# Keys and values of a fifth batch made between two decoder layers, with their weights in a free part of the transposed inputs

## The chip, the cores and the metric

The kernel runs on one core of a Trainium2 chip. The metric is the device time of one execution in microseconds (us). Times of the kernel before are the median of 3 runs. TensorE is PE in the profile, VectorE is DVE, ScalarE is ACT, GpSimd is POOL and SyncE is SP.

## What is computed

Two decoder layers over x of 16 batches, 112 tokens and 256 features, all in float32. A context of 16 x 375 x 256 feeds both cross-attentions. Each step adds to x what it makes of the normalised x:

```
x = x + L0_attn(norm(x))            # linear attention, 16 heads
x = x + L0_xattn(norm(x), ctx)      # softmax attention to the context, 16 heads of 16
x = x + L0_ffn(norm(x))             # shared expert + 2 of 16 experts per token
x = x + L1_attn(norm(x))            # softmax attention, 16 heads of 64
x = x + L1_xattn(norm(x), ctx)      # the second cross-attention
x = x + L1_ffn(norm(x))             # 2 of 8 experts, limited capacity
```

The second cross-attention makes its keys and values from the context alone, so they can be made at any time once the context is there:

```
cn = layer_norm(context, g2, b2)
kv = cn @ Wkv                       # 256 x 1024
k, v = split(kv, 2)                 # 8 heads of 64 each
out = softmax((xn @ Wq) k^T / 8) v @ Wout + bout
```

## The kernel before

x stays in SBUF for the whole kernel, tokens on the partitions. `xnT` holds the normalised x transposed (128 x 2 x 1792), made new for every step. `w_all` is one large buffer that holds the weights of the stages in turn. Nearly all matrix products of the linear layers are recorded at one line, L120 (`mm_sum`).

**What is made ahead.** For four batches, `AHEAD = (0, 4, 8, 12)` (L359), keys and values of the second cross-attention are made in layer 0, at the end of its cross-attention and during the routing and the shared expert of its feed-forward step. For each of these batches, `ctx_ahead` loads the context (L226), `norm_ahead` normalises it on VectorE (L238), `c_ahead` transposes it on PE (L389) and scales it on ScalarE into a tile `acT` (L392), `k_ahead` makes a quarter of the keys (two matmuls over 375 columns, copied by ScalarE to `ak`, L401), and `v_ahead` makes a third of the values (two matmuls over 512 columns, copied to `av`, L414). After the last piece, ScalarE's DMA queue writes `ak` and `av` to the DRAM tensors `kd` and `vd` (L403, L416), 750 KB each: `ak` has 128 partitions of 6000 bytes, `av` 125 partitions of 6144 bytes. The weights Wkv lie in `w_all` at this time (`wkv_a[0]`), and that place is later needed for W_qkv of layer 1.

**The expert blocks.** Tokens are scattered to DRAM by expert (`xg`, POOL's indirect DMA, L1063) and read back in blocks of 128 rows. `blocks(0)` (L1143) runs 36 blocks, software-pipelined: step n fetches block n + 5 (L1100, SP's queue), transposes block n (L1110, copied by VectorE at L1112), multiplies block n - 1 by its expert's weights (L120), transposes its activation for block n - 2 (L1126, copied by ScalarE at L1128), and makes the output of block n - 3 (L1133), which ScalarE scales into `os` (L1135) and POOL scatters to `yo` (L1063). The order on PE and VectorE in this stage is the one written in the code. W_qkv of layer 1 is loaded in three parts of 1 MB, behind the fetches of blocks 12, 17 and 22 (L1103). Then a branch on the number of blocks used (L1161, L1162) skips the further blocks; with these inputs they are not needed. The pools of layer 0 are closed after it, and the tiles of layer 1 are put into the memory they give back.

**Layer 1.** `combine(b)` (L1528) loads the expert outputs of batch b from `yo` (L1530, SP's queue) and adds them to x (L1533); `norm_one` normalises (statistics on VectorE, the power on POOL at L242 and L243), transposes on PE (L267) and copies into `xnT` (L269). The first four batches come ahead of the self-attention; SP loads the weights of layer 1 after the fourth.

In the second cross-attention, batch b is attended to in two units of four heads: `scores` (L1461; maxima on VectorE at L1472, exponentials on ScalarE at L1473, division by the sums on POOL at L1484), `turned` (transposes of the weights, L1493) and `values` (L1509, copied by VectorE at L1516). While batch b is attended to, keys and values of batch b + 1 are made from the context (`c_piece`, `k_piece`, `v_piece`: transposes L1430, matmuls L120, copies L1440 and L1447), or, for a batch of `AHEAD`, read from `kd` and `vd` (`k_load` L1415, `v_load` L1419, SP's queue). Here too PE's order is the written one.

Of the kernel before, what the change touches and what calls it, by code (L numbers as in the profile page):

```python
# [18 lines left out]
S = 375  # L19
KC = 125  # L20
NKC = S // KC
NT = B * L
# [76 lines left out]
def tile_decoder(ctx: ExitStack, tc: tile.TileContext, t: dict, out: bass.AP):  # L99
    nc = tc.nc  # L100
# [12 lines left out]
    def bank():  # L113
        return banks.tile([128, 512], F32, tag="B", name="pT")
# [3 lines left out]
    def mm_sum(o, terms):  # L118
        for i, (l, r) in enumerate(terms):
            mm(o, l, r, start=(i == 0), stop=(i == len(terms) - 1))  # L120
# [11 lines left out]
    xnT = xp.tile([128, 2, NT], F32, tag="xnT", name="xnT")  # L132
# [22 lines left out]
    def rows_of(w):  # L155
        return w.rearrange("(c p) n -> p c n", p=128)
# [4 lines left out]
    def load_w(at, parts):  # L161

        views, o = [], at
        for w in parts:
            c, k = w.shape[0] // 128, w.shape[1]
            v = w_all[:, o : o + c * k].rearrange("p (c n) -> p c n", c=c)
            nc.sync.dma_start(v, rows_of(w))
            views.append(v)
            o += c * k
        return views  # L170
# [46 lines left out]
    def vec(i):  # L217
        return vT[:, i : i + 1]
# [5 lines left out]
    def load_ctx(cxp, b):  # L224
        cx = cxp.tile([KC, NKC, D], F32, tag="cx", name="cx")
        nc.sync.dma_start(cx, t["ctx_1024"][b].rearrange("(c p) d -> p c d", p=KC))  # L226
        return cx
# [9 lines left out]
    def normed(dst, src, mv, r):  # L237
        nc.vector.tensor_scalar(dst, src, mv, r, ALU.subtract, ALU.mult)  # L238
# [117 lines left out]

    AHEAD = (0, 4, 8, 12)  # L359
    kd = {b: dr.tile([128, 4, S], F32, tag=f"kd{b}", name=f"kd{b}") for b in AHEAD}  # L360
    vd = {b: dr.tile([KC, NKC, 512], F32, tag=f"vd{b}", name=f"vd{b}") for b in AHEAD}

# [3 lines left out]
    acxs, acTs, akv = {}, {}, {}  # L366
    wkv_a, kap = [], []


    def ctx_ahead(i):  # L370
        if i < len(AHEAD):
            acxs[i] = load_ctx(cxp, AHEAD[i])

    def norm_ahead(i):
        for j in range(NKC):
            n = AHEAD[i] * NKC + j
            normed(acxs[i][:, j, :], acxs[i][:, j, :], cmv[:, n, 0:1], cr[:, n : n + 1])


    def c_ahead(i, c):  # L380
        if c == 0:
            acTs[i] = (
                kap[0].tile([128, 2, S], F32, tag="acT", name="acT", bufs=1)
                if i % 2
                else w_all[:, 2 * WR + 4864 : 2 * WR + 4864 + 2 * S].rearrange("p (c s) -> p c s", c=2)
            )
        pt = bank()
        for j in range(NKC):
            nc.tensor.transpose(  # L389
                pt[:, j * KC : (j + 1) * KC], acxs[i][:, j, c * 128 : (c + 1) * 128], ident[:KC, :KC]  # L390
            )
        nc.scalar.activation(acTs[i][:, c, :], pt[:, :S], AF.Identity, bias=vec(10 + c), scale=vec(8 + c))  # L392
        if c == 1:
            ctx_ahead(i + 2)

    def k_ahead(i, m):
        if m == 0:
            akv[i] = kz[0] if i == 0 else kap[0].tile([128, 4, S], F32, tag="ak", name="ak")
        pk = bank()
        mm_sum(pk[:, :S], [(wkv_a[0][:, c, m * 128 : (m + 1) * 128], acTs[i][:, c, :]) for c in range(2)])  # L400
        nc.scalar.copy(akv[i][:, m, :], pk[:, :S])  # L401
        if m == 3:
            nc.scalar.dma_start(kd[AHEAD[i]], akv[i])  # L403

    def v_ahead(i, j):
        if j == 0:
            akv[i] = (
                va[0].rearrange("p j h d -> p j (h d)")
                if i == 0
                else kap[0].tile([KC, NKC, 512], F32, tag="av", name="av")  # L410
            )
        pv = bank()
        mm_sum(pv[:KC, :], [(acTs[i][:, c, j * KC : (j + 1) * KC], wkv_a[0][:, c, 512:]) for c in range(2)])
        nc.scalar.copy(akv[i][:, j, :], pv[:KC, :])  # L414
        if j == NKC - 1:
            nc.scalar.dma_start(vd[AHEAD[i]], akv[i])  # L416

    ahead = [
        f
        for i in range(len(AHEAD))  # L420
        for f in (
            [lambda i=i, m=m: k_ahead(i, m) for m in range(4)]
            + [lambda i=i: v_ahead(i, 0)]
            + [lambda i=i, c=c: c_ahead(i + 1, c) for c in range(2)] * (i + 1 < len(AHEAD))
            + [lambda i=i, j=j: v_ahead(i, j) for j in (1, 2)]
        )
    ]
    ahead = [lambda c=c: c_ahead(0, c) for c in range(2)] + ahead

    def take(n):  # L430
# [522 lines left out]
    with ExitStack() as ph:  # L953
# [140 lines left out]
        with tc.manual_schedule(engines={mybir.EngineType.PE, mybir.EngineType.DVE}):  # L1094
            xbs, xTs, cols, acts, aTs = {}, {}, {}, {}, {}

            def fetch(j):
                if j < stop:
                    xbs[j] = lp.tile([BLK, RW], F32, tag="xb", name="xb", bufs=8)
                    got = nc.sync.dma_start(xbs[j], xg[j * BLK : (j + 1) * BLK, :])  # L1100
                    after_all("xg", got)
                    i = (j - 12) // 5
                    if j in (12, 17, 22):  # L1103
                        with tc.issue_after(got.ins):
                            w_qkv.extend(load_w(2 * WR + 2048 * i, [t["L1_attn_W_qkv"][i]]))

            def turn(j):
                pt = bank()
                for c in range(2):
                    nc.tensor.transpose(pt[:, c * BLK : (c + 1) * BLK], xbs[j][:, c * 128 : (c + 1) * 128], ident)  # L1110
                xTs[j] = lp.tile([128, 2 * BLK], F32, tag="bxT", name="bxT", bufs=3)
                nc.vector.tensor_copy(xTs[j], pt[:, : 2 * BLK])  # L1112

            def up(j):
                cols[j] = nc.tensor.value_load(ebi[0:1, j : j + 1], min_val=0, max_val=(E0 - 1) * 768)
                xt = xTs.pop(j)
                pu = bank()
                mm_sum(
                    pu[:, :256],
                    [(xt[:, c * BLK : (c + 1) * BLK], ew[:, bass.ds(cols[j] + c * 256, 256)]) for c in range(2)],  # L1120
                )
                acts[j] = swiglu(lp, pu[:, :128], pu[:, 128:256], 128)

            def turn_act(j):
                pt = bank()
                nc.tensor.transpose(pt[:, :BLK], acts.pop(j), ident)  # L1126
                aTs[j] = lp.tile([128, BLK], F32, tag="aT", name="aT", bufs=3)
                nc.scalar.copy(aTs[j], pt[:, :BLK])  # L1128

            def down(j):  # L1130
                xb = xbs.pop(j)
                po = bank()
                mm(po[:, :D], aTs.pop(j), ew[:, bass.ds(cols.pop(j) + 512, D)], start=True, stop=True)  # L1133
                os_ = lp.tile([BLK, D], F32, tag="os", name="os", bufs=8)
                nc.scalar.activation(os_, po[:, :D], AF.Copy, scale=xb[:, D + 1 : D + 2])  # L1135
                to = lp.tile([BLK, 1], U32, tag="to", name="to", bufs=8)

                own = lp.tile([BLK, 1], F32, tag="own", name="own", bufs=8)
                nc.vector.tensor_scalar(own, xb[:, D : D + 1], 2.0 * NT - 0.5, float(j * BLK), ALU.is_gt, ALU.mult)
                nc.vector.tensor_tensor(to, own, xb[:, D : D + 1], ALU.add)  # L1140
                scatter("yo", yo, to[:, 0:1], os_[:, :])

            def blocks(begin):  # L1143
                for j in range(begin, begin + 5):
                    fetch(j)
                for n in range(begin, stop + 3):
                    if n < stop:
                        fetch(n + 5)
                        turn(n)
                    if begin <= n - 1 < stop:  # L1150
                        up(n - 1)
                    if begin <= n - 2 < stop:
                        turn_act(n - 2)
                    if begin <= n - 3:
                        down(n - 3)


            w_qkv = []
            stop = NB_MEAN
            blocks(0)  # L1160
        n_used = nc.values_load(used[0:1, 0:1], min_val=0, max_val=NB0)  # L1161
        with tc.If(n_used > NB_MEAN):  # L1162
            with tc.manual_schedule(engines={mybir.EngineType.PE, mybir.EngineType.DVE}):
                stop = NB0
                blocks(NB_MEAN)
    cstack.close()
    f0s.close()
    rp = pool(ctx, "route", 1)
# [128 lines left out]
    with ExitStack() as ph:  # L1297
# [243 lines left out]
        with tc.manual_schedule(engines={mybir.EngineType.PE}):  # L1541
            for b in range(4):
                got = combine(b)
# [13 lines left out]
            for n, (g, i) in enumerate(units):  # L1557
# [7 lines left out]
                if n % 2 == 0 and n // 2 + 4 < B:  # L1565
                    got = combine(n // 2 + 4)
# [79 lines left out]
    with ExitStack() as ph:  # L1646
# [143 lines left out]
        got = {}  # L1790
# [75 lines left out]
        with tc.If(n_ranks > RANKS):  # L1866
            with tc.manual_schedule(engines={mybir.EngineType.DVE, mybir.EngineType.PE}):
# [5 lines left out]
                for i in range(len(ffn1_more)):  # L1873
                    n = len(ffn1_units) + i
# [33 lines left out]
```

## Time and profile before

| what | us |
|---|---|
| median of 3 runs (lowest to highest) | 1606.19 (1604.55 to 1608.27) |
| the profiled execution | 1611.35 |
| its span, first to last instruction | 1609.6 |
| PE busy in it | 1501.8 |
| start of the block stage's first transposes on PE | 546.60 |
| last matmul of the blocks starts | 607.10 |
| first yb load on SP | 613.90 |
| first transposes of layer 1 on PE | 620.98 |
| second cross-attention, first scores to last values' copy | 949 to 1315 |

How to read the lines: a line of a timeline has the start, the duration in us, the engine, the line of the code, the operation, what it writes and reads, the shape and the count; in brackets stands the idle time of the engine before it and what ended it. In PE's lines a float32 matmul of the code counts twice. A line of a window has the stretch, its length, the busy time of PE, PE's weight loads (PEld), VectorE, ScalarE and POOL with their instruction counts, the granted share of TensorE's clock, the busy share of the DMA engines and GB/s.

### The profile page before, as it was taken

Reading aid. Unit: us, or ns where it says so; the run is one execution under the profiler, and the core shown is the slowest. Engines: PE = TensorE matmul, PEld = TensorE weight load, DVE = VectorE, ACT = ScalarE, POOL = GpSimd, SP = SyncE. Lnnn points to the kernel's source line nnn. Section 1 sums busy time; section 2 is a strip of 40 time slices with the busy share of each in tenths; the row PEclk is TensorE's granted clock in tenths of the full one; section 3 lists DMA queues with packets and bytes.
Section 4 is the critical chain, followed back from the end, with each engine's and each line's share of the span. In section 5 each row is a group of like instructions: output and inputs, shape, how many; then the busy total and the mean of one; then the engine's idle time right before and its main releaser. Section 6 shows DMA issues by size and latency. Waiting matters only on the chain.

```text
span 1609.6 us, 30346 instructions
## 1 busy us (share of the span) xinstructions
PE 1501.8 (93%) x11438; PEld 1127.5 (70%) x11438; DVE 964.1 (60%) x2649; ACT 577.9 (36%) x1437; POOL 483.1 (30%) x647
## 2 busy tenths in 40 slices
PE   7898999999988896899999989999999978999998
PEld 5776777777754585778888756666666657788786
DVE  6986777777762353976677655566575566342124
ACT  3441444444442252223333233343434323333332
POOL 5642122222115352323333344544445420000000
PEclk9999999999999897999999999999999988999999
DMA  6500322222224476200000010101010012344421
GB/s 170 143 10 21 94 67 65 67 65 65 64 76 158 130 231 214 54 24 1 1 1 2 20 56 10 49 20 48 19 30 30 1 53 79 137 178 157 147 89 48
DMA packets 84929, 116.52 MB, mean 72 GB/s; under 512 B 13433, under 2 KB 70946, under 8 KB 84778
## 3 DMA queue, kind: packets, MB, share of 16 engines
q1 hardware_dynamic: 78690, 98.25, 20.1%
q0 software_dynamic: 3312, 8.54, 1.6%
q10 hardware_dynamic: 2776, 7.72, 1.4%
q8 instruction: 95, 1.56, 0.4%
q14 instruction: 56, 0.46, 0.1%
HBM read 84.41 MB, written 22.08 MB: 66 GB/s over the span
## 4 chain that ended last, share of the span: by engine, by line
PE 76%; DVE 13%; POOL 4%; DMA 3%; issue 2%; another core or an unknown queue 1%; ACT 1%; SPq 0%; POOLq 0%; DVEq 0%; ACTq 0%
PE pT L120 49%; PE pT L785 3%; PE pT L1461 3%; PE pT L1493 2%; POOL pr L1484 2%; DVE mx L769 2%; PE pT L1509 2%; PE pT L803 2%; PE pT L767 2%; PE pT L1358 2%; PE pT L1393 2%; PE pT L1379 2%; PE pT L620 1%; DVE st L234 1%
## 5 line engine op out<-in xcount | busy, mean ns | idle before, releaser
L1484 POOL TENSOR_SCALAR pr<-pr,den 112x375 f32<-112x375 f32 x128 | 157.0, 1244 | 176.9 <-DVE den L1482 157.7
L120 PE MATMUL pT<-xnT,w_all 128*128 128x224 f32 (+2 forms) x800 | 165.3, 358 | 0.6 <-DVE xnT L269 0.5
L120 PEld LDWEIGHTS pT<-xnT,w_all 128*128 128x128 f32 x800 | 145.9, 197 | 10.2 <-issue 5.7
L794 ACT ACTIVATE pr<-pT 125x336 f32<-125x336 f32 x256 | 94.6, 456 | 126.3 <-PE pT L785 126.3
L769 DVE TENSOR_REDUCE mx<-pT 112x1 f32<-112x375 f32 x256 | 122.2, 539 | 11.3 <-PE pT L767 9.9
L1371 POOL TENSOR_TENSOR pr<-pr,den 112x448 f32<-112x448 f32 x64 | 59.9, 956 | 198.8 <-DVE den L1369 147.9
L120 PE MATMUL pT<-w_all 128*128 (+3 forms) x376 | 113.1, 453 | 1.7 <-ACT w_all L392 0.8
L120 PE MATMUL pT<-w_all,cT 128*125 128x256 f32 (+1 forms) x336 | 111.4, 475 | 0.0
L120 PE MATMUL pT<-cT,w_all 128*128 128x375 f32 x320 | 110.2, 486 | 0.0
L120 PE MATMUL pT<-w_all,xnT 128*112 128x256 f32 (+1 forms) x320 | 105.7, 477 | 1.9 <-ACT xnT L566 0.9
L120 PE MATMUL pT<-w_all,oT 128*112 128x256 f32 x448 | 106.4, 383 | 0.6 <-DVE oT L1400 0.6
L242 POOL TENSOR_SCALAR nr<-nmv 112x1 f32<-112x1 f32 x96 | 22.3, 232 | 273.7 <-DVE nmv L235 273.1
L1308 ACT COPY pT<-pT 112x448 f32<-112x448 f32 (+1 forms) x64 | 34.0, 532 | 170.9 <-PE pT L1493 88.3
L120 PEld LDWEIGHTS pT<-w_all 128*128 128x128 f32 (+2 forms) x376 | 70.2, 190 | 33.8 <-issue 4.6
L1473 ACT ACTIVATE pr<-pT,top 112x375 f32<-112x375 f32 x128 | 72.4, 572 | 56.8 <-DVE top L1472 54.4
L120 PEld LDWEIGHTS pT<-cT,w_all 128*128 128x128 f32 x320 | 59.3, 190 | 41.1 <-issue 5.8
L120 PEld LDWEIGHTS pT<-w_all,oT 128*112 128x112 f32 x448 | 75.7, 177 | 16.3 <-DVE oT L1400 1.0
L120 PE MATMUL pT<-first_in,w_all 128*128 128x192 f32 x512 | 86.6, 329 | 0.0
L120 PEld LDWEIGHTS pT<-first_in,w_all 128*128 128x128 f32 x512 | 84.4, 192 | 1.5 <-issue 0.3
L120 PEld LDWEIGHTS pT<-w_all,cT 128*125 128x125 f32 x336 | 61.1, 187 | 33.3 <-issue 22.7
L120 PEld LDWEIGHTS pT<-w_all,xnT 128*112 128x112 f32 x320 | 57.1, 183 | 35.8 <-issue 22.4
L1767 DVE SCALAR_TENSOR_TENSOR hT<-pT,vT,gt 128x192 f32<-128x192 f32 x64 | 26.7, 417 | 90.5 <-ACT gt L1766 90.4
(306 smaller groups left out, 3019.2 us busy)
## 6 DMA issues: line engine op xcount, KB each, us to landing
w_all<-in_L_ffn_w_c_fc_dram SPq DMA_DIRECT2D x12, 1024.0 KB
w_all<-in_L_ffn_w_gate_dram SPq DMA_DIRECT2D x12, 1024.0 KB
w_all<-in_L_ffn_w_c_proj_dram SPq DMA_DIRECT2D x12, 1024.0 KB
cx<-in_ctx_dram SPq DMA_DIRECT2D x32, 375.0 KB
kz<-kn SPq DMA_DIRECT2D x128, 46.9 KB
xg<-w_all SPq DMA_DIRECT2D x1, 5547.0 KB
xb<-xg SPq DMA_DIRECT2D x36, 129.0 KB
yb<-yo SPq DMA_DIRECT2D x16, 224.0 KB
```

Of the source, the lines that this page charges most:

```text
L120: mm(o, l, r, start=(i == 0), stop=(i == len(terms) - 1))
L767: mm(ps[i][:L, :S], qz[b % 2][r, g, :], kz[b % 2][r, g, :], start=True, stop=True)
L769: nc.vector.tensor_reduce(mx[b % 2][:, g, i, 16:17], ps[i][:L, :S], AX.X, ALU.max, negate=True)
L785: mm(pw[i][:KC, j * L : (j + 1) * L], kz[b % 2][r, g, j * KC : (j + 1) * KC], qm[r, :], start=True, stop=True,)
L794: nc.scalar.activation(pr[:, i, :], pw[i][:KC, : NKC * L], AF.Exp)
L803: mm(po[32 * i : 32 * i + 32, :L], va[b % 2][:, j, 4 * g + i, :], pr[:, i, j * L : (j + 1) * L], start=(j == 0), stop=(j == NKC - 1),)
L1308: nc.scalar.copy(dst, src)
L1358: mm(ps[k][:L, s * L : (s + 1) * L], q, kk, start=True, stop=True)
L1371: nc.gpsimd.tensor_tensor(pr[:, k], pr[:, k], bcast(den[:, k, :], L), ALU.mult)
L1461: mm(ps[2 * s + k][:L, :S], qTs[b // 2][rows(k), m, (b % 2) * L : (b % 2 + 1) * L], kTs[b][rows(k), m, :], start=True, stop=True,)
L1473: nc.scalar.activation(pr[:, i, :], ps[i][:L, :S], AF.Exp, bias=top[:, i : i + 1], scale=1.0, accum_out=den[:, i : i + 1],)
L1484: nc.gpsimd.tensor_scalar(pr[:, n, :], pr[:, n, :], den[:, n : n + 1], None, ALU.mult)
```

## The change

Batch 2 becomes a fifth batch made ahead (index 4 of `AHEAD`), but not with the other four. Its weights, Wkv once more, are loaded into the last 1024 columns of `xnT`, which is free between the shared expert and batch 6 of layer 1, behind the fetch of block 24. Its context is normalised at step 30 of the blocks and transposed at steps 36 and 37, where the pipeline of the blocks runs out. Its keys are made after the last block and ahead of the branch, its values after the branch, still inside the pools of layer 0. In the second cross-attention, batch 2 is then read from `kd` and `vd` like the other batches of `AHEAD`, and its pieces during batch 1 go away.

```
-    AHEAD = (0, 4, 8, 12)
+    AHEAD = (0, 4, 8, 12, 2)
...
             acTs[i] = (
                 kap[0].tile([128, 2, S], F32, tag="acT", name="acT", bufs=1)
-                if i % 2
+                if i % 2 or i == 4
...
-        mm_sum(pk[:, :S], [(wkv_a[0][:, c, m * 128 : (m + 1) * 128], acTs[i][:, c, :]) for c in range(2)])
+        mm_sum(pk[:, :S], [(wkv_a[i // 4][:, c, m * 128 : (m + 1) * 128], acTs[i][:, c, :]) for c in range(2)])
...
-        mm_sum(pv[:KC, :], [(acTs[i][:, c, j * KC : (j + 1) * KC], wkv_a[0][:, c, 512:]) for c in range(2)])
+        mm_sum(pv[:KC, :], [(acTs[i][:, c, j * KC : (j + 1) * KC], wkv_a[i // 4][:, c, 512:]) for c in range(2)])
...
                     if j in (12, 17, 22):
                         with tc.issue_after(got.ins):
                             w_qkv.extend(load_w(2 * WR + 2048 * i, [t["L1_attn_W_qkv"][i]]))
+                    if j == 24:
+
+                        wkv_a.append(xnT[:, :, NT - 1024 :])
+                        with tc.issue_after(got.ins):
+                            nc.sync.dma_start(wkv_a[1], rows_of(t["L1_xattn_Wkv"]))
...
                     if begin <= n - 3:
                         down(n - 3)
+                    if begin == 0 and n == stop - 6:
+                        norm_ahead(4)
+                    if begin == 0 and n in (stop, stop + 1):
+                        c_ahead(4, n - stop)
...
             stop = NB_MEAN
             blocks(0)
+            for m in range(4):
+                k_ahead(4, m)
         n_used = nc.values_load(used[0:1, 0:1], min_val=0, max_val=NB0)
         with tc.If(n_used > NB_MEAN):
...
                 stop = NB0
                 blocks(NB_MEAN)
+        with tc.manual_schedule(engines={mybir.EngineType.PE}):
+            for j in range(NKC):
+                v_ahead(4, j)
     cstack.close()
     f0s.close()
```

The list of pieces that layer 0 works off stays at the first four batches; the context of batch 2 is loaded when the third of them has been transposed.

More of the change, by code (lines that the diff above doesn't have):

```diff
@@ L419, in tile_decoder @@
         f
-        for i in range(len(AHEAD))
+        for i in range(4)
         for f in (
@@ L423, in tile_decoder @@
             + [lambda i=i: v_ahead(i, 0)]
-            + [lambda i=i, c=c: c_ahead(i + 1, c) for c in range(2)] * (i + 1 < len(AHEAD))
+            + [lambda i=i, c=c: c_ahead(i + 1, c) for c in range(2)] * (i < 3)
             + [lambda i=i, j=j: v_ahead(i, j) for j in (1, 2)]
```

## The prediction

> **What bounds the kernel now.** I read the page first, then three stages that the change touches: the expert blocks, the gap between the layers, and the second cross-attention.
>
> From the page: the span, PE's share, and the chain that ended last.
>
> ```profile
> span 1609.6 us, 30346 instructions
> PE 1501.8 (93%) x11438; PEld 1127.5 (70%) x11438; DVE 964.1 (60%) x2649; ACT 577.9 (36%) x1437; POOL 483.1 (30%) x647
> ...
> PE 76%; DVE 13%; POOL 4%; DMA 3%; issue 2%; another core or an unknown queue 1%; ACT 1%; SPq 0%; POOLq 0%; DVEq 0%; ACTq 0%
> ```
>
> TensorE carries 76% of the chain. So work taken off it counts where it sets the pace, and work put on it costs nothing only where it idles. The timeline of PE at the end of the blocks shows where the change puts its work:
>
> ```profile
> 607.10 1.27 PE L1133 MATMUL pT<-w_all,aT 128*128 x4
> 620.98 0.61 PE L267 MATMUL pT<-call,xn 112*128 112x112 f32 x2 [12.61 <-DVE nmv L235]
> ```
>
> PE idles 12.6 us. What ends the idle time is a chain: the last rows of the blocks are scattered to DRAM, land, are loaded back as yb (L1530), added to x, normalised and transposed. The timeline and the waits of SP's queue:
>
> ```profile
> 613.90 5.56 SPq L1530 DMA_DIRECT2D yb<-yo  x4
> ```
> ```profile
> SPq L1530 <- DMA yo<-os,to: 13.6, 1, 13.6
> ```
>
> Whatever delays the yb load at 613.90 delays all that follows: between 613.90 and 620.98 nothing else runs. That load is the point to watch.
>
> **The change, part by part.**
>
> *In the blocks: +1.3.* The 1 MB weight load is put behind the fetch of block 24, two blocks behind the third W_qkv load. In the trace W_qkv's packets run from 577.81 to 582.06 (4.25 us), and xb 23, queued behind them, lands at 582.41, 1.43 before its transpose. Xb 24 lands at 583.23; then the new 4.1 us of packets, and xb 25 (0.85) lands near 588.1, where its transpose stands at 587.10: a stall of 1.0 (bounds 0 and 1.5). PE repeats every 1.63 us without slack, so the stall stays. The three normalisations (L238, 0.41 each) ahead of block 31's copy (L1112) take 1.2 us of VectorE, which is busy 1.02 of each 1.63 (0.29, 0.15, 0.16, 0.42); the copy, needed 1.0 after it would end, comes 0.25 late: +0.3 (0 to 0.6). The extra ctx load (375 KB) follows the third context's transposes, before 500; nobody needs it before 595: 0 (at most 1).
>
> *The drain: +0.6 ahead of K.* ScalarE gets two acT (L392, 0.665 each) among the last aT and os. From 607.35 its queue is acT, aT 0.27, os 0.47, acT, os 0.47. So the second acT ends near 609.5 (block shift left out) and the last os near 610.0 instead of 608.88. That os still makes its scatter: POOL issues the last three at a 1.26 pitch, the last at 610.40.
>
> *The fill on PE.* In the second cross-attention the same pieces take, by their starts on PE (half a batch's K at 985.59, then a third of V up to the values at 989.93, all of it PE work without a gap):
>
> ```profile
> 981.65 0.86 PE L1430 MATMUL pT<-call,cx 125*128 125x125 f32 x6
> ...
> 985.59 2.69 PE L120 MATMUL pT<-cT,w_all 128*128 128x375 f32 x8
> 988.12 1.88 PE L120 MATMUL pT<-w_all,cT 128*125 128x512 f32 x4
> 989.93 1.37 PE L1509 MATMUL pT<-pT,vt 125*64 125x112 f32 x24
> ```
>
> So 0.70 for the transposes, 2.53 + 2.62 for K, 1.81 + 3.43 for V: 11.1 in all. K runs 609.5 to 614.65, its last copy (0.47) ends near 615.1. The branch is cheap: in the trace ScalarE's last os ends at 608.88 and its block-end semaphore comes at 609.49, so 0.6; the first V matmul waits for that: 615.7. V ends at 620.95, its last copy (L414, 0.585) at 621.6. The PE work itself fits the gap to within 0.1.
>
> *The new wait: this decides.* The pools of layer 0 close behind the fill, and the yb tiles come from memory that is given back there. In the built program SP's first yb load waits, beside the scatters as before, for ScalarE's last av copy and for the two DMA lanes on which batch 2's kd and vd writes land. Behind it stand on SP all of yb 1 to 3 and the L1 weights; POOL (bout), VectorE (x + yb) and PE (L267) wait for the same set. How long does a vd write take? The trace holds one nearly alone: issued at 545.90, last packet at 553.05, 7.15 us. The kd write of the same 750 KB, issued at 528.2, ended at 531.42, 3.2 us. Two windows over their packets (DMA share and GB/s stand last):
>
> ```profile
> 546.70:553.00 6.30, 5.23 (x28) 3.89 (x27) 2.98 (x10) 1.16 (x6) 0.00 (x0) 1.00 0.30 118
> ...
> 529.10:531.40 2.30, 2.30 (x7) 1.61 (x6) 0.69 (x1) 0.00 (x0) 1.88 (x2) 0.50 1.00 367
> ```
>
> The vd write keeps 0.30 of the DMA engines busy, kd all. I take 7.15, the row of the same shape; 3.2 is the other end. So vd lands at 621.65 + 7.15 = 628.8, and the yb load goes out 0.3 later, its place in the wait list: 629.1. Against 613.90 that is +15.2, with the blocks' shift **+16.5** (bounds: 12.5 with kd's 3.2; 20 with V and the restart at half clock as below).
>
> *The clock.* Granted clock is the third number from the end:
>
> ```profile
> 607.71:611.12 3.41, 0.66 (x3) 0.26 (x2) 0.00 (x0) 0.95 (x2) 2.63 (x3) 1.00 0.32 123
> 611.12:614.53 3.41, 0.00 (x0) 0.00 (x0) 0.00 (x0) 0.00 (x0) 0.25 (x1) 0.50 0.10 38
> ...
> 624.77:628.19 3.42, 3.42 (x11) 3.09 (x10) 1.22 (x4) 0.54 (x1) 1.58 (x4) 0.50 1.02 396
> 628.19:631.60 3.41, 3.41 (x20) 3.41 (x19) 0.62 (x1) 0.54 (x1) 0.00 (x0) 1.00 1.07 383
> ```
>
> A 3.41 us window with little PE work is followed by half clock, and it came back 7.2 us after PE restarted at 620.98. K and V follow a busy drain, so I give them the full clock. The 1.2 us between them may drop V's clock for a window: 0 taken, 1.7 as bound. [...] But V ends 15 us before the new restart, so PE goes cold again and the restart costs what it cost: 0.
>
> *In the second cross-attention: -5.4.* Batch 2 loses 11.1 of PE work while batch 1 is attended to. But without it POOL's weights division (L1484, 4 x 1.22 per unit) sets the pace, as it does before batch 4:
>
> ```profile
> 1039.80 4.87 POOL L1484 TENSOR_SCALAR pr<-pr,den 112x375 f32<-112x375 f32 x4 [3.95 <-DVE den L1482]
> ...
> 1041.10 0.58 PE L1493 MATMUL pT<-call,pr 112*125 112x112 f32 x3 [0.83 <-POOL pr L1484]
> ```
>
> The copies of L1516 close each unit. Batches 1 and 2 run from 978.83 to 1025.63, 46.8; batches 3 and 4, the nearest pair whose second is loaded ready, to 1067.37, 41.7: 5.1 less. Later pairs: 49.0 and 48.9 made, 42.5 and 41.5 loaded, but they hold other routing work. Pair 3 and 4 has one router matmul more (0.3): I take 5.4, bounds 4.4 and 11.1 (POOL no bound). The two loads go out on SP when the buffers come free (scores end near 960, values near 968), 20 us before they are needed; other loads pass behind them without haste.
>
> **Sum.** +16.5 - 5.4 = +11.1. The profiled execution took 1611.35 (span 1609.6 and 1.75 around it), so 1622.5; it lay 5.2 above the median of the runs, 1606.19, and by the median the forecast is **1617.3**.
>
> **Rivals.**
> 1. *The gap hides the fill* (faster). If the yb load did not wait for vd's landing, the blocks' 1.3 and the gain would be left: 1.3 - 5.4 = -4.1, so 1602.1. For it: K and V fit 12.6 us. Against: the wait stands in the built program. It turns at a hold of the yb load of 4.1 us; I find 15.2. Chance 0.04.
> 2. *Cold fill, or a slow write.* V at half clock, vd beside other traffic or a worse restart: +3 to +6 more, 1620 to 1623.5. For: clock rows above. Chance 0.14, mostly in the range.
> 3. *POOL does not limit batch 1*, or vd takes kd's 3.2: 11.1 - 5.7 = 5.4, or 11.1 - 4.0 = 7.1 more than before, so 1611.6 to 1613.3. Against: the rows of batch 4 and of vd. Chance 0.08.
> 4. *It comes out even*: the hold is half of what I find and the gain at its best. Chance 0.02.
>
> The forecast has 0.72. The range, 1611.0 to 1623.5, takes in rivals 2 and 3. What can be told from no change is 0.2%, 3.2 us: faster 0.04, within 0.02, slower 0.94.
>
> **What would show it.** In the profile of the changed kernel: the first yb load near 630 instead of 613.90, released by a vd write or by ScalarE's av copy; vd issued near 623 and 0.30 DMA share for 6 us behind it; PE idle about 15 us again, now behind V; half clock over the restart; xb 25 released by its DMA; POOL waits in batch 1 like those of batch 4, and batches 1 and 2 near 41. I am wrong if SP issues the first yb load before vd lands, or if batch 1 sheds the whole 11.1.

## The result, and the profile after

The changed kernel takes **1621.15 us** (median of 8 runs, 1613.66 to 1627.22), the kernel before, run beside it, 1605.80 (8 runs, 1603.34 to 1613.48). The ratio is 1.0081, 95% interval 1.0060 to 1.0103: **slower by 13 us** by this ratio and by 15.4 by the medians, where 11.1 were forecast. Four runs of the changed kernel lie at 1614 to 1617 us, at a mean granted clock of 0.971 to 0.974, and four at 1626 to 1627, at 0.965 to 0.968, so that the median stands between them, where no run is; both profiles that were taken of it (1615.98, and 1614.82 later) are like the first four.

The profiled execution of before reached the blocks 7 to 10 us later than those below, ahead of anything that the change touches. So stages are compared below with another profile: that of the kernel before with one word changed, which makes no difference (own_bytes_before, first experiment). All times are stretches between starts of the same instructions in the traces, in us:

| stretch | own_bytes_before | after | after again |
|---|---|---|---|
| first block's transpose to the last down | 63.90 | 65.08 | 64.58 |
| last down to the first yb load | 5.69 | **20.58** | **20.60** |
| yb load to the first scores of layer 1 | 24.81 | 25.25 | 25.76 |
| these scores, first to last | 292.99 | 293.12 | 293.40 |
| second cross-attention, batches 1 and 2 | 46.80 | **42.85** | **42.88** |
| batches 3 and 4 | 44.77 | 41.77 | 41.77 |
| first block's transpose to the end | 1065.9 | 1077.1 | 1075.0 |

The last row gives +11.2 and +9.1, against the forecast +11.1. One profile against one carries some 3 us of chance. Before's own profile takes 1062.8 over the last row's stretch, and against that it is +14.3 and +12.2. Its blocks, the first row, take 60.99, and those of l1_again (below), which has the same code up to there, 66.7. Its batches 3 and 4 take 41.75 with 3.4 us of half clock in them, where the control's 44.77 have 10.2.

First the page of after: span, PE's share, and the chain by engine.

```profile
span 1614.2 us, 30350 instructions
...
PE 1505.7 (93%) x11438; PEld 1129.8 (70%) x11438; DVE 962.7 (60%) x2646; ACT 579.6 (36%) x1440; POOL 483.6 (30%) x647
...
PE 51%; DVE 5%; POOL 4%; DMA 1%; ACT 1%; issue 1%; POOLq 0%; ACTq 0%; DVEq 0%; SPq 0%
```

PE's 93% has not moved, and the kernel is 13 us slower: the share does not tell it. The chain's shares sum to 63% where those of before summed to 100%: the walk back stopped early, so they can't be compared.

The timeline of after in the gap, all engines (start, length, engine, line, what; in brackets the idle time before, and what ended it):

```profile
602.66 5.21 PE L120 MATMUL pT<-acT,xnT 128*128 128x375 f32 x16
...
609.05 5.42 PE L120 MATMUL pT<-xnT,acT 128*125 128x512 f32 x12 [1.19 <-ACTq L1173]
609.12 0.35 ACTq L403 DMA_DIRECT2D kd<-ak  x1
...
614.51 0.58 ACT L414 COPY av<-pT 125x512 f32<-125x512 f32 x1 [1.13 <-PE pT L120]
615.12 0.50 ACTq L416 DMA_DIRECT2D vd<-av  x1
622.81 5.15 SPq L1544 DMA_DIRECT2D yb<-yo  x4
623.45 0.61 POOL L1315 DMA_DIRECT2D bout<-in_L_xattn_bout_dram  x1 [18.01 <-DMA vd<-av]
...
629.26 0.61 PE L267 MATMUL pT<-call,xn 112*128 112x112 f32 x2 [14.79 <-DVE nmv L235]
```

K (602.66) and V (609.05) fill the gap as forecast, the vd write goes out at 615.12, and for 7.7 us nothing is issued. Then yb (622.81) and bout (623.45) go out together; POOL's line names what they waited for, `vd<-av`. SP's own waits view names another releaser for the same time:

```profile
SPq L1544 <- DMA yo<-os,to: 15.6, 1, 15.6
```

That is the trap of a wait for several semaphores: the scatters (`yo<-os,to`) are in the same list, but the last was issued at 604.47. Who waits at the same moment for the same set, here POOL, helps to tell. The window over vd's packets in after (DMA share and GB/s last):

```profile
616.00:622.20 6.20, 0.00 (x0) 0.00 (x0) 0.00 (x0) 0.00 (x0) 0.00 (x0) 0.67 0.30 119
```

0.30 of the DMA engines, no engine computing: the row of the earlier vd write once more.

### The profile page after: what moved, and what is told of

Its sections match the earlier page's. It is cut to its first block, busy times and chain, and to the rows that moved or that the text cites. A ratio compares the mean times of both kernels' runs of the same rounds, so it can differ in the third digit from the quotient of the medians.

```text
span 1614.2 us, 30350 instructions
## 1 busy us (share of the span) xinstructions
PE 1505.7 (93%) x11438; PEld 1129.8 (70%) x11438; DVE 962.7 (60%) x2646; ACT 579.6 (36%) x1440; POOL 483.6 (30%) x647
## 3 DMA queue, kind: packets, MB, share of 16 engines
q1 hardware_dynamic: 79236, 100.83, 20.6%
## 4 chain that ended last, share of the span: by engine, by line
PE 51%; DVE 5%; POOL 4%; DMA 1%; ACT 1%; issue 1%; POOLq 0%; ACTq 0%; DVEq 0%; SPq 0%
PE pT L120 35%; POOL pr L1498 3%; PE pT L1475 3%; PE pT L1507 2%; PE pT L1523 2%; PE pT L1372 2%; PE pT L1407 2%; PE pT L1393 2%; PE pT L1821 1%; PE pT L1289 1%; DVE x_res L1547 1%; ACT pr L1487 1%; PE pT L1444 1%; PE pT L267 1%; POOL pr L1385 0%
## 5 line engine op out<-in xcount | busy, mean ns | idle before, releaser
L1498 POOL TENSOR_SCALAR pr<-pr,den 112x375 f32<-112x375 f32 x128 | 157.1, 1245 | 174.1 <-DVE den L1496 155.1
L120 PE MATMUL pT<-w_all,cT 128*125 128x256 f32 (+1 forms) x324 | 105.9, 471 | 0.0
L120 PE MATMUL pT<-cT,w_all 128*128 128x375 f32 x304 | 104.6, 485 | 0.0
L1322 ACT COPY pT<-pT 112x448 f32<-112x448 f32 (+1 forms) x64 | 34.1, 532 | 170.5 <-PE pT L1507 88.1
```

What stands on the lines that cost most here:

```text
L1322: nc.scalar.copy(dst, src)
L1498: nc.gpsimd.tensor_scalar(pr[:, n, :], pr[:, n, :], den[:, n : n + 1], None, ALU.mult)
```

## The experiments

The theory is that of the prediction: the yb load waits until batch 2's vd write has landed, because its tile lies in memory that layer 0's pools give back. Rivals: the fill's own work is the cost; the writes' traffic is; the second cross-attention gains nothing. A ratio is always against the kernel before on the same chip, with its 95% interval.

### The wait taken away: own_bytes, and its control own_bytes_before

```diff
-        lp = pool(ph, "a1", 2)
+        lp = pool(ph, "a1", 2, reuse_waits="tile")
```

With this a tile of layer 1's first pool waits only for the users of its own bytes, not for every user of the pools that lay there. Nothing else is edited. The control has the same line in the kernel before.

> The changed kernel, with the tiles of the second layer's first pool waiting only for the users of their own bytes. The first yb load then waits for the scatters alone; fill, writes and loads stay. Theory (the hold: the yb load waits for batch 2's vd write): the yb load goes out about 6 us behind the last down instead of 20.6, PE restarts right behind V's last matmul (near 615 in a profile like that of after, instead of 629), and the time falls by 12 to 15 from the changed kernel's, to 2 to 6 below the kernel before; if the restart finds the full clock, up to 6 more. Rival 1 (the fill's own work on PE and ScalarE is the cost, the yb load only one of several that end together): the restart moves by less than 6 and the time stays above the kernel before. Rival 2 (the yb rows are late because the writes of kd and vd take the DMA engines): the load goes out early but takes much longer than 5 us.

> The kernel before with the same one word on the pool, nothing else. It tells what that word does alone. In before the first yb load waits for the last scatter's landing and ScalarE's last os, which is done by then: every theory expects no change, 0 within 1.5 us, and the yb load about 6 us behind the last down as before.

Measured: own_bytes **1.0014** (0.9991 to 1.0038; 1607.1 against 1607.7), control 0.9997 (0.9982 to 1.0012). The yb load goes out 7.07 behind the last down instead of 20.58, and 0.67% of the 0.81% is gone, by one wait. So the wait is the cost, and the fill's work on PE is not: late_kd, below, bounds that work at 1.2 behind the last down, and ahead of it the transposes of the context add 0.4 (from block 35's transposes to the last down 4.47 instead of 4.08). Rival 1 falls. But 2 to 6 us below the kernel before were expected, and the time does not go below it. Part of this is seen in the gap. SP's and PE's timelines of own_bytes:

```profile
608.77 8.77 SPq L1544 DMA_DIRECT2D yb<-yo  x4
```
```profile
608.52 5.42 PE L120 MATMUL pT<-xnT,acT 128*125 128x512 f32 x12 [1.18 <-ACTq L1173]
618.79 0.63 PE L267 MATMUL pT<-call,xn 112*128 112x112 f32 x2 [4.85 <-DVE xn L238]
```

and the same load in the control:

```profile
609.32 4.83 SPq L1530 DMA_DIRECT2D yb<-yo  x4
```

Four loads of 224 KB hold SP for 8.77 instead of 4.83, because kd's packets (609.45 to 612.28) stand in front of them, and PE restarts 4.85 behind V. Rival 2, the traffic, has its share: from the yb load to the first scores 28.66 instead of 24.81.

### A faster vd write: v_split

```diff
-            nc.scalar.dma_start(vd[AHEAD[i]], akv[i])
+            nc.scalar.dma_start(vd[AHEAD[i]][:112], akv[i][:112])
+            nc.scalar.dma_start(vd[AHEAD[i]][112:], akv[i][112:])
```

(for batch 2 alone)

> The changed kernel with batch 2's vd write cut in two: rows 0 to 111, and rows 112 to 124. The bytes and the waits stay. Theory (the hold ends with the vd write, and that write is slow because its 125 rows go over 0.30 of the DMA engines): the two parts take about 3.5 instead of 7.15 from the issue, the yb load comes 3 to 4 us earlier and the time falls by 3 to 4. Rival 1 (the write is slow by itself, 750 KB to DRAM behind kd's): still about 7, no change. Rival 2 (the hold ends with something else than the write): the write is faster, the yb load does not move.

Measured: **1.0056** (1.0037 to 1.0075), 0.25% or 4 us better than the changed kernel's ratio, with intervals that overlap (1.0075 and 1.0060). The two parts go out at 619.41 and 619.77, their last packet ends at 623.25, and yb follows 17.2 behind the last down instead of 20.6. A window over their packets, and SP's timeline:

```profile
620.30:623.20 2.90, 0.00 (x0) 0.00 (x0) 0.00 (x0) 0.00 (x0) 0.00 (x0) 1.00 0.79 250
```
```profile
623.73 5.24 SPq L1548 DMA_DIRECT2D yb<-yo  x4
```

The same bytes at 0.79 of the DMA engines instead of 0.30. The write takes 3.84 from its first issue instead of 7.15, and the yb load comes 3.4 earlier: in the trace the dose follows, in the run times its sign does. Kd's write of 128 rows keeps 0.81 of them busy (after, 609.90 to 612.30). Why 125 rows in one write keep so few busy, and 112 with 13 beside them so many, is not shown.

### The cost alone: fill_only

```diff
-        own = [b for b in range(B) if b not in AHEAD]
+        own = [b for b in range(B) if b not in AHEAD[:4]]
```

(and the same in the two conditions that choose between making and loading a batch)

> The changed kernel with everything in the fill (weights loaded, K and V of batch 2 made and written), but the second layer makes batch 2 again by itself, as before, and does not read the written one. It shows the cost without the gain. Theory: the hold of 14.5 and the blocks' 0.6 remain and the 4 of the second cross-attention are not gained: 14 to 16 above the kernel before, 3.5 to 5 above the changed kernel. Rival (the second cross-attention gains nothing in the end, the copy of 4 is lost later): the same time as the changed kernel.

Measured: **1.0110** (1.0093 to 1.0128), 17.7 us, where 14 to 16 were expected. In its profile yb follows 20.60 behind the last down, and batches 1 and 2 take 46.81. The hold is as in the changed kernel and the loaded batch's gain is absent. In run time the two differ by 0.3%, with intervals that overlap (1.0093 and 1.0103): the sign fits the theory, the size is not settled.

### The gain alone: l1_only, and l1_again for a second profile

```diff
-            nc.sync.dma_start(kTs[b], kd[b])
+            nc.sync.dma_start(kTs[b], kd[0 if b == 2 else b])
```

(vd likewise, and batch 2 counted among those that are loaded)

> The kernel before, in which batch 2's keys and values of the second cross-attention are not made but loaded from batch 0's in DRAM: the gain without the cost. It leaves out the making of batch 2's K and V, so batch 2 attends to batch 0's context. Theory: batches 1 and 2 take 42.8 instead of 46.8 because POOL's division sets the pace, and the time falls by 4 to 5.4. Rival 1 (POOL does not set the pace): by 8 to 11. Rival 2 (what is gained there is lost behind it, the whole stage waits for something else): by less than 2.

> l1_only once more, for another profile. It leaves out the making of batch 2's K and V. Its twelve runs had a median of 1609.0, with a mean granted clock of 0.963 to 0.970 in eleven of them; the profiled one was the twelfth, 1594.3 at 0.975. Theory (POOL's division sets the pace where the next batch is loaded, PE idles there, and the granted clock falls to a half behind windows in which PE was busy less than about 2 of 3.41 us, so that the gain is paid back): the profile of a run near 1609 has more or longer half-clock stretches in the second cross-attention than that of 1594, 10 us of them or more, and the stage from the first values copy on is longer by the difference. Rival (the time is lost before the second cross-attention, in the first layer or the gap): the half-clock stretches there are the same, and the difference stands elsewhere.

Measured: l1_only **1.0013** (1.0002 to 1.0025): no gain at all, where 4 to 5.4 us were expected; l1_again one run, 1607.11 beside 1605.7. In both profiles batches 1 and 2 take what was expected, 42.93 and 41.78. So the work is saved where it should be, and the time is lost elsewhere. The two profiles, of 1594.3 and of 1607.1, show one place: the end of layer 1's self-attention, in windows that lie on the clock's own grid of 3.41 us (PE busy, then the granted clock). First the execution of 1594.3:

```profile
916.73:920.14 3.41, 2.86 (x32) 1.00 0.00 0
920.15:923.56 3.41, 1.96 (x32) 1.00 0.10 16
923.56:926.97 3.41, 2.73 (x17) 1.00 0.33 133
926.97:930.38 3.41, 1.67 (x20) 1.00 0.19 81
930.39:933.80 3.41, 2.93 (x17) 1.00 0.00 0
```

and that of 1607.1:

```profile
922.78:926.19 3.41, 2.36 (x32) 1.00 0.00 0
926.19:929.60 3.41, 1.77 (x22) 1.00 0.27 90
929.60:933.01 3.41, 3.41 (x11) 0.50 0.34 138
933.02:936.43 3.41, 1.47 (x20) 1.00 0.01 2
936.43:939.84 3.41, 3.41 (x13) 0.50 0.00 0
```

The same instructions, cut otherwise by the grid: in the one PE's idle time is spread over the windows and the clock stays, in the other it falls together and two windows run at half clock. Between 900 and 1250 the first has 17.1 us of half clock, the second 34.1; from the last scores of the self-attention to unit 25 of the second cross-attention they take 311.4 and 319.3. Half of 17 is 8.5, and 7.9 is the difference. The kernel before takes 315.2 over this stretch, its control 318.6: in the one profile of l1_only the gain is there, in the other it is gone. But the two half-clock windows above stand ahead of batch 1, in work that the edit leaves as it was. That loading batch 2 brings them about is not shown; why all but two of the twelve runs took 1607 to 1612 is open. The rest of the 12.8 lies in the blocks (2.9, an xb load that lands late at block 18), in the self-attention (1.2) and in what follows.

### Idle matmuls where PE is thin: l1_spin and late_spin

```diff
+        def spin(k):
+            sp = bank()
+            for _ in range(k):
+                mm(sp[:, :S], wkv[:, 0, :128], wkv[:, 0, :S], start=True, stop=True)
...
+                    if thin and j == NKC - 1 and i < 3:
+                        spin(1)
...
+                if n >= 29:
+                    spin(3)
                 pT = turned1(pr)
```

`thin` holds in the units next to a batch that is loaded. late_spin has this on late_kd_load27 (below).

> l1_only (batch 2's K and V left out, batch 0's read in their place) with idle matmuls on PE, 128x375 each, whose result nobody reads: one behind each head's transposes in the units where the next batch is loaded, where PE waits 0.63 for POOL at each, and three ahead of the transposes of the last three units of the self-attention, where PE waits 1.0 to 1.9. Theory (the gain of the loaded batch is paid back by the granted clock, which falls to a half behind thin windows): the half-clock stretches behind these places go, the mean granted clock of the runs rises from 0.963 to 0.970 to 0.973 or more, and the median falls from 1609 to between 1594 and 1602. Rival 1 (the clock falls for another reason): the stretches stay, the median moves by less than 2. Rival 2 (the added matmuls stand in PE's way): 2 to 6 slower.

> late_kd_load27 with the same idle matmuls: the whole change with its hold taken away, kd's write behind V, the load at block 27. Theory: what the second cross-attention gains is kept, 1597 to 1604, below the kernel before by 3 to 9. Rival 1: no change from late_kd_load27's 1608.6. Rival 2: slower by 2 to 6.

Measured: l1_spin **0.9952** (0.9933 to 0.9971), late_spin **0.9975** (0.9960 to 0.9990), the only two below the kernel before, by work that is added to PE. (This chip was slower: before 1614.3.) The mean granted clock of the runs is 0.971 to 0.979 and 0.975 to 0.983, where before has 0.968 to 0.973 beside them. In l1_spin's profile only 6.8 us between 900 and 1250 are at half clock, in late_spin's 3.4. Batches 1 and 2 take 40.55 and 40.54. PE in l1_spin, where batch 2 begins (L1490 are the idle matmuls):

```profile
999.67 0.58 PE L1498 MATMUL pT<-call,pr 112*125 112x112 f32 x3
1000.09 0.81 PE L1490 MATMUL pT<-w_all 128*128 128x375 f32 x2
1000.73 0.56 PE L1498 MATMUL pT<-call,pr 112*125 112x112 f32 x3
1001.13 0.81 PE L1490 MATMUL pT<-w_all 128*128 128x375 f32 x2
```

They stand in the time in which PE waited for POOL (0.24 to 0.84 a head in after, from 1001.48 on). In windows on the clock's grid the same place of l1_spin reads:

```profile
997.95:1001.36 3.41, 3.41 (x36) 1.00 0.00 0
1001.36:1004.77 3.41, 3.41 (x18) 1.00 0.03 5
```

and that of after, without the idle matmuls:

```profile
996.97:1000.38 3.41, 3.41 (x38) 1.00 0.00 0
1000.38:1003.79 3.41, 1.42 (x12) 1.00 0.00 0
1003.79:1007.20 3.41, 3.06 (x10) 0.50 0.02 5
1007.21:1010.62 3.41, 3.41 (x16) 0.50 0.00 0
```

So in after the loaded batch's own units bring on half clock, and the idle matmuls take it away. From the last scores of the self-attention to unit 25, l1_spin takes 311.5 and late_spin 310.0, as the better profile of l1_only does. That half clock is what hid the gain in the run times of l1_only fits this, but is not shown by itself, since the matmuls stand next to other batches and in the self-attention too. What these matmuls would do in the kernel before, which has thin units of its own at batches 4, 8 and 12, was not tried; how much of the 0.5% belongs to batch 2 is open.

### The gap cleared: late_kd, and the load five blocks on: late_kd_load27

late_kd is own_bytes with batch 2's kd write behind V's last copy; the write between K and V is left out:

```diff
+                with tc.issue_after(last.ins):
+                    nc.scalar.dma_start(kd[AHEAD[i]], late_k[0])
             nc.scalar.dma_start(vd[AHEAD[i]], akv[i])
```

late_kd_load27 has `if j == 27:` for `if j == 24:` ahead of the weight load as well.

> own_bytes with batch 2's kd write issued behind V's last copy, ahead of the vd write, instead of between K and V. In own_bytes the first four yb loads moved their packets from 611.02 to 617.07 beside and behind kd's 750 KB (609.45 to 612.28), where they took 610.29 to 612.10 for the first two without it, and PE restarted 4.9 us behind V. Theory (the hold is gone, but the write in front of the loads took its place): the first two yb land within 3 us of their issue, PE restarts 1 to 2 us behind V's last matmul, and the time falls by 2.5 to 4 from own_bytes', to 2.5 to 4 below the kernel before. Rival (PE work of V in the gap sets the restart): restart unchanged, 4.9 us behind V, and no change from own_bytes. A miss that is possible: both writes now stand in front of yb 2 and 3 and of the weights, and 1 to 2 us come back there.

> late_kd with the 1 MB weight load behind the fetch of block 27 instead of 24, five blocks behind the third W_qkv load, as those stand to one another. In the profiles with the load at 24 the blocks 23 to 26 took 5.3 to 6.4 instead of 4.88. Theory (the load's packets stand in front of xb 25): those steps go back to 1.63 each, the blocks end 0.4 to 1.5 earlier, the time falls by as much from late_kd's. Rival (the slow steps come from the copies and normalisations, or from xb's own loads): the same steps are late elsewhere, no change.

Measured: **1.0011** (0.9990 to 1.0033) and **1.0016** (0.9999 to 1.0033). PE in late_kd:

```profile
611.00 5.42 PE L120 MATMUL pT<-xnT,acT 128*125 128x512 f32 x12 [1.18 <-ACTq L1178]
617.29 0.41 PE L267 MATMUL pT<-call,xn 112*128 112x112 f32 x2 [0.88 <-DVE xn L238]
```

The restart stands 0.88 behind V instead of 4.85, as expected, and from the last down to the first scores late_kd takes 31.7 where own_bytes takes 35.7 and the control 30.5. The gap is cleared to about 1 us. But the 4 us are not in the run time: a miss of the expectation. late_kd's profile has 34.1 us of half clock between 900 and 1250 where own_bytes' has 23.9, and half-clock windows at the self-attention's end like those of l1_again. The load at 27 made blocks 23 to 35 take 19.66 in one profile (late_kd 20.71) and 24.84 in another. That is late_spin's, where the weight load's packets take 7.0 us, PE waits 2.47 for xb 28 and a half-clock window follows. So it is no cure.

### The load alone: load_only

```diff
+                    if j == 24:
+                        with tc.issue_after(got.ins):
+                            nc.sync.dma_start(xnT[:, :, NT - 1024 :], rows_of(t["L1_xattn_Wkv"]))
```

> The kernel before, with the 1 MB weight load behind the fetch of block 24, and nothing that uses it. Theory: xb 25 lands late, 0.4 to 1.5 us more between blocks 23 and 26, and the time rises by as much; it may not be told from no change. Rival (the loads behind it, yb and the layer's weights, are also late): 3 or more.

Measured: 1.0011 (0.9998 to 1.0024). Blocks 23 to 35 take 19.53 in four of the five profiles without the load (19.82 in l1_spin), 20.97 here, and 20.1 to 21.2 in the six others with the load at 24. These six hold the three normalisations too, and 0.12 is theirs: the step behind block 32 takes 1.75 or 1.76 instead of 1.63 in all eight profiles that have them, and in no other. That leaves 0.4 to 1.6 for the load.

### The changed kernel again: after_again

No edit.

> The changed kernel once more, for another profile: its eight runs lie at 1614 to 1617 (three, clock 0.971 to 0.974) and at 1626 to 1627 (five, clock 0.965 to 0.968), and the profiled one was of the first kind. Theory: a run of the second kind differs by half-clock stretches in the second layer, above all behind the units where batch 2 and the other loaded batches are attended to; the hold of the yb load is the same 20.6 behind the last down in both. Rival: the hold differs by 10 us.

Measured: 1614.82 beside 1605.7, so again not a run near 1626, of which there were four and not five. The hold is the same 20.60. v_split's profile (1624.55, clock 0.968) has the pattern of l1_again: half clock from 944.7, 951.5 and 968.6, 38.3 instead of 34.0 from the last scores to the first values copy (34.0 is after's). That the changed kernel's 1626 come from this too is likely, not shown.

## Why the prediction was right, and where it was not

- **The hold: right.** Forecast 15.2 from a vd write of 7.15; the write took 7.15 (615.12 to 622.27), yb went out 14.5 to 14.9 later than without it. Taking the wait away and making the write faster moved the yb load by 13.5 and 3.4; the ratio fell by 0.67% (10.8 us) and by 0.25%, the latter within the intervals.
- **The fill on PE: right.** K 5.21 (5.15 forecast), V 5.42 (5.24), 1.2 between them for the branch (1.05).
- **The blocks: right,** +1.3 forecast, 0.6 to 1.7 measured over blocks 23 to 35. The load's part is 0.4 to 1.6 for 1.0. The normalisations cost 0.12 in every profile that has them, where 0.3 were forecast.
- **The clock at the restart: right** as 0: 25.25 and 25.76 against 24.81, with 17.1 us of half clock as in before.
- **The gain: mis-sized.** The step was "POOL's weights division sets the pace", -5.4, from the pair of batches 3 and 4. The stage gave -3.95 and -3.92. POOL does pace those units (in after PE waits 0.84, 0.63, 0.63 and 0.24 for L1498 at the four heads from 1001.48 on), but it also leaves PE so thin (1.42 of 3.41) that the clock falls, and 6.8 us of the pair run at half. With one such window (l1_again, late_kd) the pair takes 41.8, with two 42.9, with three (v_split) 45.0, with none and idle matmuls 40.55. The measure, 41.7 for batches 3 and 4, was itself a profile with one such window; the control and load_only, with three, take 44.8 and 44.9. The clock was weighed in the gap alone and not here.
- **The sum: right within its range, closer in part by luck.** Against the control the profiles give 11.2 and 9.1 for 11.1, but batches 3 and 4, in which the control had more half clock, take 3.0 off that; against before's own profile they give 14.3 and 12.2. The runs give 13 by the ratio and 15.4 by the medians, 2 to 4 more than forecast: 1.5 is the gain's, the rest is not assigned. A part depends on how the clock's grid cuts the later stages, which no term of the sum had. The median, 1621.15, is inside the range though the four runs near 1626 are above its end, 1623.5.
- **Rival 1** (the gap hides the fill) fell as built. Its condition, no wait for vd's landing, was then made in own_bytes, and the -4.1 it promised did not come either. Kd's traffic took about 4 of it in the gap, as late_kd shows; with that gone it did not come in late_kd either, where half clock is likely the reason and not shown to be.
- **Rivals 2 and 3** did not come, though the time lies in the 1620 to 1623.5 of rival 2: V ran at full clock (5.42), the vd write took neither more than 7.15 nor kd's 3.2, and the pair shed 3.9 of the 11.1.

## What to carry to other kernels

Work put into a gap is not free because it fits: look at what its last write holds, above all which memory is given back behind it, and let the next pool wait by its own bytes, or keep the write away from what the path needs next. Before PE's work is taken away in a stage that another engine paces, look at what its clock will do there: here half-clock windows took back 1.2 to 4.5 of the 6.2 us that the pair of batches could shed, and idle matmuls kept them. With gains of a few us, test the gain alone and the cost alone: here the cost stood at 1.1% by itself, and the gain at nothing. And take more than one profile of a kernel, since a stage that serves as a measure (here 41.7) can be 3 us longer in the next.

## What the hardware showed that was not expected

The granted clock follows PE's busy time in windows of 3.41 us, and not only where PE idles a whole window: in after, a window with 1.42 busy is followed by half clock from 1003.79 on. The windows keep one grid through the execution: in after, half clock starts at 119.74, 536.17, 1003.79 and 1328.06, the last three 122, 259 and 354 windows of 3.413 us behind the first. Over the 14 profiles, from 600 us to 1580, of the windows at full clock:

| PE busy in the window | windows | half clock in the next |
|---|---|---|
| under 1.50 of 3.41 | 63 | 62 |
| 1.50 to 2.25 | 106 | 65 |
| 2.25 and more | 3495 | 0 |

So here half clock begins behind windows that are about half busy. And 17 us of it, the difference of l1_only's two profiles between 900 and 1250, are worth 8.5 us by an estimate (half of 17, since in after the eight matmuls of L1475 take 1.52 at full clock, 995.94, and 2.85 at half, 1006.01; the two profiles differ by 7.9 from the last scores of the self-attention to unit 25) or 0.5% of the span, where the largest effect of any edit here was 1.1%. Between 1.50 and 2.25 the modelled busy time alone does not tell which way it goes.

A second thing: loads of 224 KB beside a 750 KB write were held back well after the write's last packet. In own_bytes the first two yb took from 611.02 to about 616, the write's last packet having ended at 612.28, where the control's took 1.8 us (610.29 to 612.10). Bout's packets (112 KB) ran from 612.38 to 615.16 there, beside 1.5 us in late_kd; what holds them all in that time was not found.
